# Graph attention in four layers: attention logits from 8-column products ahead of the value projection

## The chip, the cores and the metric

The kernel runs on one core of a Trainium2 chip. The metric is the device time of one execution in microseconds (us), taken as the median of several runs. A core has a matrix engine (TensorE, PE in the profile, with its weight loads shown apart as PEld), a vector engine (VectorE, DVE), a scalar engine for functions of one argument (ScalarE, ACT), a general engine (GpSimd, POOL) and a queue that issues transfers (SyncE, SP). Each runs its own instructions in the order in which they were written and waits on semaphores for the others. Products land in PSUM[...]; everything else lies in SBUF.

## The reference

Sixteen graphs of 1024 nodes with 256 features, each with a 0/1 adjacency matrix, go through four layers of graph attention. Every layer first normalises the features and clips them at zero, and adds its result to its input:

```python
h = jnp.maximum(_layernorm(x, axis=-1), 0.0)
x = x + _L0_gnn_ref(h, adj, L0_gnn_W, L0_gnn_a)
```

Within a layer, with H heads (4, 4, 4, 1) of 256/H columns:

```python
h = (x @ W)                                   # the values
s1 = einsum('bhnd,hd->bhn', h, a1)            # one number s per node and head
s2 = einsum('bhmd,hd->bhm', h, a2)            # one number d per node and head
e = leaky_relu(s1[:, :, :, None] + s2[:, :, None, :], slope)
e = where(adj == 0, -inf, e)
out = einsum('bhnm,bhmd->bhnd', softmax(e), h)
```

Layer 2 adds a bias, a clip, the values and a second normalisation over each head. Layer 3 has one head of 256 columns. All in float32.

## The kernel before, in words

*Numbers of a node.* The weights `wa[layer]` hold, per head, the columns of W and two more: W times a1 and W times a2 (line 579; folded in `weights`, lines 685 to 689). One product of the normalised features with `wa` so gives values and the logits' s and d together: 4 x 66 = 264 columns for four heads, 258 for one. Since a leaky ReLU of a sum is a maximum of two sums, the exponential of a logit can be written as a factor of the column node times (a row value relative to a threshold, clipped at zero, plus a constant). The factors `fac` (per column node) and the `rows` (per row node, spread over all partitions) come from s and d, less their maxima over all nodes.

*Units and tiles.* A unit is one layer of one graph. The 48 units of layers 0 to 2 stand in an order `main`, two graphs interleaved; each has 32 tiles (4 heads x 8 blocks of 128 column nodes). A tile goes through three engines: ACT makes `r` of 128 x 1024 in PSUM (`weigh`, line 991; two buffers), DVE adds, multiplies by the mask and writes `p` to SBUF (`cover`, line 1009; 13 buffers), PE multiplies `p` with the values `v` into `po` (`gather`, line 1075). `evacuate` and `finish` divide by the sums and update `x_cur`, the latter on POOL. The 16 units of layer 3 (`last_layer`, line 1178; `last_sums`, line 1193) run beside the tiles of other units.

*Preparing a unit* (`prepare`, line 801) starts at the earliest AHEAD = 60 tiles before its first tile and after the graph's former layer is finished. DVE takes the statistics (`st`), POOL turns them into offset and scale (`rs`), and then for four pairs of blocks (`normal`, line 750): POOL writes `hn`, PE transposes it, ACT clips it into `hT` (three buffers), and two `project` jobs (line 777) multiply `hT` with `wa` into a PSUM bank and copy the result to `v`. When the last of eight blocks is copied (`not u.left`, line 853), DVE reduces s and d over the node blocks (tile `wide`), PE transposes that, DVE reduces to the maximum over all nodes (`top`), PE spreads it with a product with `ones`, and DVE computes the exponents (`c`, `arg`) from s and d. ACT takes exponentials into `wide` (row side) and `fac`. The row side is transposed and goes through DRAM (`line`) to be read back over all partitions as `rows`; the very first unit and the last unit of layer 3 make it with PE instead (`direct`, line 917). In layers 0 and 1, POOL multiplies the values by a factor (`flatten`, line 959); otherwise it sets the column of ones in `v`.

*Order.* The file holds a planner (class `Plan`, line 417; main loop, line 1343): at build time it runs through all jobs with assumed durations (`cost`, line 437), picks for each engine among the jobs that can start first (within NEAR = 60 ns) the one with the smallest `until`, and emits instructions in that order. A preparation's `until` is the number of its unit's first tile; a gather's is the current tile plus SLACK = 36. Copies marked EITHER go to ACT as long as it isn't a nanosecond count of 10^9 behind DVE (DVE_MORE, line 389), which means always. PSUM has two banks `pp` for transposes, projections, the small products and the last layer's sums, two of twice the size for `r`, and two for `po`.

Of the kernel before, what the change touches and what calls it, by code (L numbers as in the profile page):

```python
# [20 lines left out]
P = 128  # L21
# [388 lines left out]
POOL_LATE = 100.0  # L410
LANES = 2


# [3 lines left out]
class Plan:  # L417
# [19 lines left out]
    def cost(self, engine: str, op: str, a: tuple, k: dict):  # L437
        size = lambda ap: math.prod(ap.shape[1:])
        aps = [v for v in (*a, *k.values()) if hasattr(v, "shape")]
        n = max(size(v) for v in aps)  # L440
        if engine == "PE":
            out, left = a[0], a[1]
            wide = size(left) > 64
            swap = 110.0 if self.mode not in (None, wide) else 0.0
            self.mode = wide
            if op == "transpose":
                return swap + (110.0 if left.dtype == F32 else 56.0), PE_LATE
            if left.dtype != F32:
                return swap + 57.0, PE_LATE
            return swap + max(59.0, size(out) * 0.833 + 3.0), PE_LATE  # L450
        if op == "dma_start":
            total = math.prod(a[0].shape) * mybir.dt.size(a[0].dtype)
            return (600.0 if engine == "POOL" else 400.0), 2200.0 + total / 180.0
        given = sum(size(v) == 1 for v in aps)
        if engine == "ACT":
            if n == 1024:
                return (1041.0 if "accum_out" in k else (903.0, 1050.0, 1143.0)[given]), ACT_LATE
            if n <= 64:
                return 100.0 + 0.7 * n, ACT_LATE
            return 50.0 + 0.833 * n + 114.0 * given + (40.0 if given == 2 else 0.0), ACT_LATE  # L460
# [48 lines left out]
def fast_path(  # L509
# [44 lines left out]
    WIDTH = [F // n + 2 for n in HEADS]  # L554
    VW = max(n * w for n, w in zip(HEADS, WIDTH))
    MAXN = max(HEADS)
# [193 lines left out]
    def normal(e, rs: bass.AP):  # L750
# [20 lines left out]
        else:  # L771
            dve.tensor_scalar(e.hT, ph.rearrange("p k i n -> p k (i n)"), 0.0, None, ALU.max)
        left()
        for i in range(2):
            add(u.until, project(e, i), plan.now)

    def project(e, i: int):

        u = e.u
        width = u.n * (u.w + 2)  # L780
        yield "PE", lambda: u.layer in folded and free_for(u) and max(folded[u.layer], free_for(u))
        pv, left = bank_for(u)
        for k in range(KC):
            for c in range(0, P, P // 2):
                at = i * P + c
                pe.matmul(
                    pv[c : c + P // 2, :width],
                    e.hT[:, k, at : at + P // 2],
                    wa[u.layer][:, k, :, :].rearrange("p h e -> p (h e)"),
                    start=(k == 0),  # L790
                    stop=(k == KC - 1),
                )
        e.left -= 1
        e.read = plan.now
        yield EITHER, None
        either_copy(u.v[:, 2 * e.pair + i, :width], pv[:, :width])
        left()
        u.left -= 1
        u.there = plan.now

    def prepare(u: "Unit"):

        n, w, layer = u.n, u.w, u.layer
        slope = SLOPE[layer]
        width = n * (w + 2)
        yield "DVE", lambda: (
# [7 lines left out]
        else:  # L814
            u.v = units.tile([P, NB, width], F32, name="v_one", bufs=1)
        v = u.v[:, :, :width].rearrange("p b (h e) -> p b h e", h=n)
        plan.now = max(plan.now, u.g.here)
        xt = u.g.x
        st = small.tile([P, NB, 2, 3], F32, name="st", bufs=2)
        for i in range(NB):  # L820
# [4 lines left out]

        rs = small.tile([P, 6, NB], F32, name="rs", bufs=2)
        m0, m1, q0, q1 = st[:, :, 0, 1], st[:, :, 1, 1], st[:, :, 0, 2], st[:, :, 1, 2]
# [9 lines left out]
        for pair in range(NB // 2):  # L837
            yield "POOL", lambda: (
                (len(pairs) < TURNS or pairs[-TURNS].turned)
                and (len(pairs) < PAIRS or not pairs[-PAIRS].left)  # L840
                and max(
                    1.0,
                    pairs[-TURNS].turned if len(pairs) >= TURNS else 0.0,
                    pairs[-PAIRS].read if len(pairs) >= PAIRS else 0.0,
                )
            )
            e = Unit()
            e.u, e.pair, e.turned, e.left = u, pair, False, 2
            pairs.append(e)
            g = normal(e, rs)  # L850
            add(u.until, g, 0.0, next(g))

        yield "DVE", lambda: not u.left and u.there
        s, d = (v[:, :, :, w + c].rearrange("p b h -> p h b") for c in range(2))

# [4 lines left out]
        mx = mine[:, 1, : 2 * n].rearrange("p (c h) -> p c h", c=2)  # L860
        dve.tensor_reduce(mx, v[:, :, :, w : w + 2].rearrange("p b h c -> p c h b"), AX.X, ALU.max)
        yield "PE", free_bank
# [11 lines left out]
        yield "DVE", None  # L874
        c = small.tile([P, 7, MAXN], F32, name="c", bufs=2)
        S, D, t, c1, c2, b1, b3 = (c[:, i, :n] for i in range(7))
# [82 lines left out]
    def flatten(u: "Unit", v: bass.AP):  # L959

        flat = u.fac[:, 2].rearrange("p h b -> p b h")
        for b in range(0, NB, 2):
# [28 lines left out]
    def weigh(u: "Unit", h: int, j: int):  # L991

        r, k = wide_bank()
        base = -1.0 if u.shared else u.fac[:, 3, h, j : j + 1]
        act.activation(r, u.row[h][0], AF.Relu, bias=base, scale=u.fac[:, 1, h, j : j + 1])
        weighed.append((u, None, h, j, r, k, plan.now))

    def weigh_some(u: "Unit", i: int, j: int):
# [5 lines left out]
        for k in range(MANY):  # L1004
            scale = u.fac[:, 1, 0, j + k : j + k + 1]
            act.activation(r[:, k], of, AF.Relu, bias=u.fac[:, 3, 0, j + k : j + k + 1], scale=scale)
        weighed.append((u, i, 0, j, r, at, plan.now))

    def cover():
# [3 lines left out]
        if i is None:  # L1013
            base = 1.0 if u.shared else u.fac[:, 2, h, j : j + 1]
            dve.scalar_tensor_tensor(by_blocks(p), by_blocks(r), base, mask(u.g, j), ALU.add, ALU.mult)
            covered.extend((u, c, h, j, p[:, c * half_n : (c + 1) * half_n], k, plan.now) for c in range(2))
        else:
            p_holds[k] = MANY
            p = p.rearrange("p (k n) -> p k n", k=MANY)
            for c in range(MANY):  # L1020
                m = mask(u.g, j + c)[:, i]
                dve.scalar_tensor_tensor(p[:, c], r[:, c], u.fac[:, 2, h, j + c : j + c + 1], m, ALU.add, ALU.mult)
                u.ps.append((p[:, c], k, plan.now))
# [4 lines left out]
    def make_whole(u: "Unit", h: int, j: int):  # L1028

        p, k = numerators()  # L1030
        whole[0] += 1
        base = -1.0 if u.shared else u.fac[:, 3, h, j : j + 1]
        act.activation(p, u.row[h][0], AF.Relu, bias=base, scale=u.fac[:, 1, h, j : j + 1])
        yield "POOL", None
        pool.tensor_scalar(p, p, 1.0 if u.shared else u.fac[:, 2, h, j : j + 1], 1.0, ALU.add, ALU.mult)
        yield "POOL", None
# [38 lines left out]
    def gather():  # L1075
# [7 lines left out]
        po = g[0]  # L1083
        at = h * (w + 2)
        for q in range(QUAD):
# [42 lines left out]
    def finish(u: "Unit", h: int, att, total):  # L1128

        n, w = u.n, u.w  # L1130
        at = h * (w + 2)
        wide = lambda ap: ap.unsqueeze(2).to_broadcast([P, NB, w])
# [134 lines left out]
    for b in range(G):  # L1267
# [4 lines left out]
        for layer in range(LAYERS):  # L1272
            u = Unit()
            u.g, u.layer, u.n, u.w = g, layer, HEADS[layer], F // HEADS[layer]
            u.finished, u.row, u.weighed, u.spent, u.left = {}, [], 0, False, NB
            u.ps = []
# [207 lines left out]
```

## Time and profile before

| | us |
|---|---|
| median of 3 runs (lowest, highest) | 3018.09 (3017.86, 3025.92) |
| the profiled execution's own time | 3014.36 |
| its span, from first to last instruction | 3012.4 |
| PE busy | 2694.6 |
| DVE busy | 2650.3 |
| ACT busy | 2414.9 |
| POOL busy | 1571.0 |
| value projection on PE (matmuls on `wa` and `hT`) | 518.3 |

All times in the profile are us, unless ns stands there. A group line names line, engine, operation, what is written and read, the shape, the count, then the busy time and the mean of one in ns, then the engine's idle time just before those instructions and who ended it. Nearly all instructions carry line 487, the helper that the planner calls them through, so groups are told apart by tile names. A line of waits has the waiting engine and tile, the releaser, total us, count and longest. A line of the timeline has the start, the time from the first start to the last end, engine, operation and count. A float32 product of 64 output rows shows as two matmuls and two weight loads.

### The profile page before, as it was taken

The page shows a single profiled execution, that of the slowest core. Times are in us where ns is not written, and L with a number is a line of the kernel's source. Part 1 is how long each engine was busy: PE and PEld are TensorE (multiplying, and loading weights), DVE is VectorE, ACT ScalarE, POOL GpSimd, SP SyncE. Part 2 cuts the span into 40 slices and gives each one's busy share as a digit, 9 for nine tenths or more (in the row PEclk, how much of TensorE's full clock was granted, in tenths as well). Part 3 has the DMA queues.
Part 4 walks back from the last instruction along what each step waited for, and adds up shares of the span by engine and source line. Part 5 has one row for each costly group of instructions (what it writes and reads, how often), then busy time and mean ns, then how long its engine had stood idle before and what let it go on. Part 6 is the DMA issues. An engine that isn't in the chain of part 4 may idle for free.

```text
span 3012.4 us, 130240 instructions
## 1 busy us (share of the span) xinstructions
PE 2694.6 (89%) x58915; PEld 2262.8 (75%) x58915; DVE 2650.3 (88%) x4065; ACT 2414.9 (80%) x3201; POOL 1571.0 (52%) x2263
## 2 busy tenths in 40 slices
PE   5888889999998989999898998989989899999867
PEld 4777777787776778778787786878778778887745
DVE  5889899899978989898998989989898998999963
ACT  5898888888878788888879788897888879878641
POOL 3445682754736447375463745637375464463630
PEclk8999999999999999999999999999999999999978
DMA  7323211323122131413113141321413213111100
GB/s 139 73 59 73 64 36 55 70 65 83 52 52 74 64 68 55 90 44 82 52 63 76 38 96 38 78 59 61 83 42 80 57 62 73 49 48 49 39 12 28
DMA packets 144292, 186.91 MB, mean 62 GB/s; under 512 B 80760, under 2 KB 116336, under 8 KB 142704
## 3 DMA queue, kind: packets, MB, share of 16 engines
q1 hardware_dynamic: 141680, 161.71, 18.5%
q0 software_dynamic: 2048, 16.78, 5.7%
q8 instruction: 464, 7.60, 1.0%
q14 instruction: 100, 0.82, 0.1%
HBM read 194.38 MB, written 34.40 MB: 76 GB/s over the span
## 4 chain that ended last, share of the span: by engine, by line
PE 35%; DVE 29%; ACT 21%; POOL 7%; issue 5%; DMA 1%; SPq 0%; ACTq 0%; POOLq 0%; DVEq 0%
DVE p L487 19%; PE pp L487 19%; PE po L487 16%; ACT r L487 15%; DVE st L487 3%; POOL att L487 2%; ACT seen L487 2%; DVE att L487 2%; ACT att L487 1%; DVE s L487 1%; DVE c L487 1%; POOL rs L487 1%; POOL hn L487 1%; ACT v L487 1%; ACT hT L487 1%
## 5 line engine op out<-in xcount | busy, mean ns | idle before, releaser
L487 ACT ACTIVATE r<-rows,fac 128x1024 f32<-128x1024 f32 (+1 forms) x1552 | 1766.0, 1148 | 363.3 <-DVE p L487 339.3
L487 PEld LDWEIGHTS po<-v,p 128*64 128x64 f32 x49216 | 1598.1, 140 | 332.4 <-DVE p L487 150.6
L487 PE MATMUL po<-v,p 128*64 128x65 f32 x49216 | 1665.0, 225 | 202.0 <-DVE p L487 128.7
L487 DVE SCALAR_TENSOR_TENSOR p<-r,mask 128x1024 f32<-128x1024 f32 x1024 | 1220.5, 1217 | 112.2 <-ACT r L487 86.8
L487 DVE SCALAR_TENSOR_TENSOR p<-r,fac,mask 128x1024 f32<-128x1024 f32 (+1 forms) x768 | 817.9, 1098 | 88.3 <-ACT r L487 71.0
L487 PE MATMUL pp<-wa,hT 128*64 128x264 f32 (+1 forms) x4056 | 518.3, 391 | 13.6 <-ACT hT L487 10.2
L487 POOL TENSOR_TENSOR att<-att,inv 128x512 f32<-128x512 f32 x128 | 133.9, 1046 | 744.6 <-DVE inv L487 628.3
L487 PE MATMUL pp<-v_one,p 128*64 128x257 f32 x3584 | 430.7, 383 | 2.7 <-DVE p L487 1.8
L487 PEld LDWEIGHTS pp<-wa,hT 128*64 128x64 f32 x4056 | 269.3, 138 | 138.9 <-ACT hT L487 16.5
L487 PEld LDWEIGHTS pp<-v_one,p 128*64 128x64 f32 x3584 | 267.2, 138 | 95.2 <-DVE p L487 9.0
L487 POOL TENSOR_SCALAR hn<-x_cur,rs 128x256 f32<-128x256 f32 x512 | 281.6, 562 | 36.4 <-PE pp L487 22.3
L487 PE MATMUL pp<-ident,hn 128*128 128x128 f32 x1020 | 178.8, 295 | 63.5 <-POOL hn L487 51.8
L487 POOL TENSOR_TENSOR x_cur<-att,x_cur 128x512 f32<-128x512 f32 x190 | 226.3, 1191 | 14.9
L487 ACT ACTIVATE r<-rows_one,fac 128x512 f32<-128x512 f32 x240 | 183.4, 778 | 19.3 <-DVE p L487 9.9
L487 PEld LDWEIGHTS pp<-ident,hn 128*128 128x128 f32 x1020 | 108.4, 143 | 120.3 <-POOL hn L487 91.9
L487 DVE BATCH_NORM_STATS2 st<-x_cur 128x6 f32<-128x256 f32 x512 | 180.8, 410 | 11.9 <-DMA x_cur<-in_x_dram 10.2
L487 ACT ACTIVATE hT<-pp 128x512 f32<-128x512 f32 x255 | 147.7, 594 | 39.3 <-PE pp L487 37.9
L487 ACT COPY v<-pp 128x264 f32<-128x264 f32 (+1 forms) x395 | 146.3, 383 | 21.1 <-PE pp L487 18.9
L487 POOL TENSOR_TENSOR v<-v,fac 128x512 f32<-128x512 f32 x128 | 136.1, 1088 | 47.3 <-ACT fac L487 47.3
L487 POOL TENSOR_TENSOR att<-att,s 128x512 f32<-128x512 f32 x124 | 133.1, 1074 | 10.0
L487 ACT ACTIVATE seen<-mask 128x1024 bf16<-128x1024 fp8e4 x128 | 134.6, 1052 | 0.4
L487 POOL TENSOR_TENSOR rs<-st 128x8 f32<-128x8 f32 x192 | 37.9, 211 | 153.9 <-DVE st L487 138.8
(91 smaller groups left out, 1616.3 us busy)
## 6 DMA issues: line engine op xcount, KB each, us to landing
rows<-line SPq DMA_DIRECT2D x191, 512.0 KB
x_cur<-in_x_dram SPq DMA_DIRECT2D x32, 512.0 KB
near<-in_adj_dram POOLq DMA_DIRECT2D x64, 256.0 KB, 8.1
out_dram<-y SPq DMA_DIRECT2D x128, 128.0 KB
rows_one<-line SPq DMA_DIRECT2D x15, 512.0 KB
mask<-near SPq DMA_TRANSPOSE x64
wa<-in_L_gnn_W_dram SPq DMA_DIRECT2D x6, 128.0 KB
line<-row SPq DMA_DIRECT2D x48, 16.0 KB
```

The source lines that it names most:

```text
L487: r = call(*a, **k)
```

## The change

The value projection no longer carries s and d. A new job `logits` runs once per pair, right after `hT`: eight products of `hT` with the two extra columns of every head (8 columns in layers 0 to 2, 2 in layer 3), all into one bank, one copy to a new small tile `sd`. The two `project` jobs of the pair multiply with the value columns alone (256), copy to `v`, and get an `until` that lies BEHIND = 16 tiles later. The maximum and the exponents read `sd` and wait for the four logits jobs (`u.begun == NB`) in place of the values. What needs the values on POOL (`flatten`, or the column of ones) waits for them there; `u.ready`, which lets ACT begin the unit's tiles, is set before that. `v` has one column per head less, `fac` one plane less (its unused first), `st`, `rs` and `c` have a third buffer. The planner's assumed cost of a product of at most 16 columns goes from 59 to 30 ns.

```diff
+BEHIND = 16
...
-            return swap + max(59.0, size(out) * 0.833 + 3.0), PE_LATE
+            return swap + (30.0 if size(out) <= 16 else max(59.0, size(out) * 0.833 + 3.0)), PE_LATE
...
-    VW = max(n * w for n, w in zip(HEADS, WIDTH))
+    VW = max(n * (w - 1) for n, w in zip(HEADS, WIDTH))
...
+        add(u.until, logits(e), plan.now)
         for i in range(2):
-            add(u.until, project(e, i), plan.now)
+            add(u.until + BEHIND, project(e, i), plan.now)
+
+    def logits(e):
+
+        u = e.u
+        yield "PE", lambda: u.layer in folded and free_for(u) and max(folded[u.layer], free_for(u))
+        pd, left = bank_for(u)
+        pd = pd[:, : 2 * 2 * u.n].rearrange("p (i h c) -> p i h c", i=2, c=2)
+        for i in range(2):
+            for k in range(KC):
+                for c in range(0, P, P // 2):
+                    at = i * P + c
+                    pe.matmul(
+                        pd[c : c + P // 2, i],
+                        e.hT[:, k, at : at + P // 2],
+                        wa[u.layer][:, k, :, u.w :],
+                        start=(k == 0 and i == 0),
+                        stop=(k == KC - 1),
+                        skip_group_check=True,
+                    )
+        e.left -= 1
+        e.read = plan.now
+        yield EITHER, None
+        either_copy(u.sd[:, 2 * e.pair : 2 * e.pair + 2], pd)
+        left()
+        u.begun += 2
+        u.known = plan.now
 
     def project(e, i: int):
...
+        pv = pv[:, :F].rearrange("p (h e) -> p h e", h=u.n)
...
-                    pv[c : c + P // 2, :width],
+                    pv[c : c + P // 2, :],
                     e.hT[:, k, at : at + P // 2],
-                    wa[u.layer][:, k, :, :].rearrange("p h e -> p (h e)"),
+                    wa[u.layer][:, k, :, : u.w],
...
-        either_copy(u.v[:, 2 * e.pair + i, :width], pv[:, :width])
+        either_copy(u.v[:, 2 * e.pair + i, : u.n * (u.w + 1)].rearrange("p (h e) -> p h e", h=u.n)[:, :, : u.w], pv)
...
+        u.sd = small.tile([P, NB, n, 2], F32, name=f"sd{n}", bufs=3)
...
-        st = small.tile([P, NB, 2, 3], F32, name="st", bufs=2)
+        st = small.tile([P, NB, 2, 3], F32, name="st", bufs=3)
...
-            e.u, e.pair, e.turned, e.left = u, pair, False, 2
+            e.u, e.pair, e.turned, e.left = u, pair, False, 3
...
-        yield "DVE", lambda: not u.left and u.there
-        s, d = (v[:, :, :, w + c].rearrange("p b h -> p h b") for c in range(2))
+        yield "DVE", lambda: u.begun == NB and u.known
+        s, d = (u.sd[:, :, :, c].rearrange("p b h -> p h b") for c in range(2))
...
-        dve.tensor_reduce(mx, v[:, :, :, w : w + 2].rearrange("p b h c -> p c h b"), AX.X, ALU.max)
+        dve.tensor_reduce(mx, u.sd.rearrange("p b h c -> p c h b"), AX.X, ALU.max)
...
-        u.fac = small.tile([P, 4, n, NB], F32, name=f"fac{n}", bufs=3)
+        u.fac = small.tile([P, 3, n, NB], F32, name=f"fac{n}", bufs=3)
...
-            act.activation(u.fac[:, 1:3], arg[:, 1:3], AF.Exp)
-            yield "POOL", None
+            act.activation(u.fac[:, 0:2], arg[:, 1:3], AF.Exp)
+            if not u.shared:
+                yield "POOL", None
+                pool.tensor_scalar(u.fac[:, 2], u.fac[:, 1], -1.0, 0.0, ALU.mult, ALU.add)
+            u.ready = plan.now
+            yield "POOL", lambda: not u.left and u.there
             if u.shared:
                 add(u.until, flatten(u, v), plan.now)
             else:
                 pool.memset(v[:, :, :, w], 1.0)
-                pool.tensor_scalar(u.fac[:, 3], u.fac[:, 2], -1.0, 0.0, ALU.mult, ALU.add)
                 u.flat = plan.now
-            u.ready = plan.now
```

The remaining edits follow the new numbering of `fac` and the narrower `v`.

More of the change, by code (lines that the diff above doesn't have):

```diff
@@ L773, in normal @@
         left()
+        add(u.until, logits(e), plan.now)
         for i in range(2):
-            add(u.until, project(e, i), plan.now)
+            add(u.until + BEHIND, project(e, i), plan.now)
[23 more added lines that the diff above has]
+        u.known = plan.now
     def project(e, i: int):
         u = e.u
-        width = u.n * (u.w + 2)
         yield "PE", lambda: u.layer in folded and free_for(u) and max(folded[u.layer], free_for(u))
         pv, left = bank_for(u)
+        pv = pv[:, :F].rearrange("p (h e) -> p h e", h=u.n)
         for k in range(KC):
@@ L804, in prepare @@
         slope = SLOPE[layer]
-        width = n * (w + 2)
+        width = n * (w + 1)
         yield "DVE", lambda: (
@@ L824, in prepare @@
         yield "POOL", None
-        rs = small.tile([P, 6, NB], F32, name="rs", bufs=2)
+        rs = small.tile([P, 6, NB], F32, name="rs", bufs=3)
         m0, m1, q0, q1 = st[:, :, 0, 1], st[:, :, 1, 1], st[:, :, 0, 2], st[:, :, 1, 2]
@@ L874, in prepare @@
         yield "DVE", None
-        c = small.tile([P, 7, MAXN], F32, name="c", bufs=2)
+        c = small.tile([P, 7, MAXN], F32, name="c", bufs=3)
         S, D, t, c1, c2, b1, b3 = (c[:, i, :n] for i in range(7))
@@ L959, in flatten @@
     def flatten(u: "Unit", v: bass.AP):
-        flat = u.fac[:, 2].rearrange("p h b -> p b h")
+        flat = u.fac[:, 1].rearrange("p h b -> p b h")
         for b in range(0, NB, 2):
@@ L993, in weigh @@
         r, k = wide_bank()
-        base = -1.0 if u.shared else u.fac[:, 3, h, j : j + 1]
-        act.activation(r, u.row[h][0], AF.Relu, bias=base, scale=u.fac[:, 1, h, j : j + 1])
+        base = -1.0 if u.shared else u.fac[:, 2, h, j : j + 1]
+        act.activation(r, u.row[h][0], AF.Relu, bias=base, scale=u.fac[:, 0, h, j : j + 1])
         weighed.append((u, None, h, j, r, k, plan.now))
@@ L1004, in weigh_some @@
         for k in range(MANY):
-            scale = u.fac[:, 1, 0, j + k : j + k + 1]
-            act.activation(r[:, k], of, AF.Relu, bias=u.fac[:, 3, 0, j + k : j + k + 1], scale=scale)
+            scale = u.fac[:, 0, 0, j + k : j + k + 1]
+            act.activation(r[:, k], of, AF.Relu, bias=u.fac[:, 2, 0, j + k : j + k + 1], scale=scale)
         weighed.append((u, i, 0, j, r, at, plan.now))
@@ L1013, in cover @@
         if i is None:
-            base = 1.0 if u.shared else u.fac[:, 2, h, j : j + 1]
+            base = 1.0 if u.shared else u.fac[:, 1, h, j : j + 1]
             dve.scalar_tensor_tensor(by_blocks(p), by_blocks(r), base, mask(u.g, j), ALU.add, ALU.mult)
@@ L1021, in cover @@
                 m = mask(u.g, j + c)[:, i]
-                dve.scalar_tensor_tensor(p[:, c], r[:, c], u.fac[:, 2, h, j + c : j + c + 1], m, ALU.add, ALU.mult)
+                dve.scalar_tensor_tensor(p[:, c], r[:, c], u.fac[:, 1, h, j + c : j + c + 1], m, ALU.add, ALU.mult)
                 u.ps.append((p[:, c], k, plan.now))
@@ L1031, in make_whole @@
         whole[0] += 1
-        base = -1.0 if u.shared else u.fac[:, 3, h, j : j + 1]
-        act.activation(p, u.row[h][0], AF.Relu, bias=base, scale=u.fac[:, 1, h, j : j + 1])
+        base = -1.0 if u.shared else u.fac[:, 2, h, j : j + 1]
+        act.activation(p, u.row[h][0], AF.Relu, bias=base, scale=u.fac[:, 0, h, j : j + 1])
         yield "POOL", None
-        pool.tensor_scalar(p, p, 1.0 if u.shared else u.fac[:, 2, h, j : j + 1], 1.0, ALU.add, ALU.mult)
+        pool.tensor_scalar(p, p, 1.0 if u.shared else u.fac[:, 1, h, j : j + 1], 1.0, ALU.add, ALU.mult)
         yield "POOL", None
@@ L1083, in gather @@
         po = g[0]
-        at = h * (w + 2)
+        at = h * (w + 1)
         for q in range(QUAD):
@@ L1130, in finish @@
         n, w = u.n, u.w
-        at = h * (w + 2)
+        at = h * (w + 1)
         wide = lambda ap: ap.unsqueeze(2).to_broadcast([P, NB, w])
@@ L1274, in fast_path @@
             u.g, u.layer, u.n, u.w = g, layer, HEADS[layer], F // HEADS[layer]
-            u.finished, u.row, u.weighed, u.spent, u.left = {}, [], 0, False, NB
+            u.finished, u.row, u.weighed, u.spent, u.left, u.begun = {}, [], 0, False, NB, 0
             u.ps = []
```

## The prediction

> **What bounds the kernel now.** I read the page first: shares, chain, groups.
>
> ```profile
> span 3012.4 us, 130240 instructions
> PE 2694.6 (89%) x58915; PEld 2262.8 (75%) x58915; DVE 2650.3 (88%) x4065; ACT 2414.9 (80%) x3201; POOL 1571.0 (52%) x2263
> PE 35%; DVE 29%; ACT 21%; POOL 7%; issue 5%; DMA 1%; SPq 0%; ACTq 0%; POOLq 0%; DVEq 0%
> L487 PE MATMUL pp<-wa,hT 128*64 128x264 f32 (+1 forms) x4056 | 518.3, 391 | 13.6 <-ACT hT L487 10.2
> ```
>
> No engine bounds it alone: three stand at 80 to 89%, and the chain that ended last changes between them. The fourth line is the value projection that the change splits. So I cut one period of the steady part (181 us, from 2187.9 to 2369.2: three units of heads and one last layer) into stretches of 7.5 us; five of them:
>
> ```profile
> core 0: us, PE busy (x) PEld busy (x) DVE busy (x) ACT busy (x) POOL busy (x), PEclk, DMA share, GB/s
> 2202.90:2210.40 7.50, 7.50 (x129) 5.55 (x127) 7.47 (x9) 7.22 (x11) 4.28 (x9) 1.00 0.01 2
> 2307.90:2315.40 7.50, 7.50 (x109) 5.22 (x103) 6.26 (x6) 6.96 (x12) 7.07 (x17) 1.00 0.60 105
> 2315.40:2322.90 7.50, 7.50 (x126) 5.85 (x126) 6.48 (x14) 7.50 (x12) 2.18 (x4) 1.00 0.77 81
> 2345.40:2352.90 7.50, 6.90 (x175) 5.89 (x171) 4.86 (x8) 7.36 (x14) 2.23 (x2) 1.00 0.21 77
> 2352.90:2360.40 7.50, 4.02 (x54) 2.43 (x54) 6.23 (x9) 7.47 (x11) 0.00 (x0) 0.89 0.00 0
> ```
>
> The first three hold preparations of a next unit (transposes, hT, values): PE is full and ACT nearly. The last two hold none: PE has room, ACT has not.
>
> Then the waits: is a unit's preparation ever late?
>
> ```profile
> ACT r L487 <- DVE c L487: 7.9, 4, 5.3
> ACT r L487 <- DMA rows<-line: 4.8, 1, 4.8
> DVE wide L487 <- ACT v L487: 36.9, 10, 17.0
> ```
>
> ACT waits 12.7 us in all for a unit's row or factors. The third line, the wait that the change shortens (the maximum over the logits waits for the last value), has two long members, seen in order of time at both ends:
>
> ```profile
> 28.27 0.27 DVE L487 TENSOR_REDUCE wide<-v 128x8 f32<-128x64 f32 x1 [17.05 <-ACT v L487]
> 35.96 2.15 ACT L487 ACTIVATE r<-rows,fac 128x1024 f32<-128x1024 f32 x2 [4.59 <-DVE rows L487]
> 2935.82 0.18 DVE L487 TENSOR_REDUCE wide<-v 128x2 f32<-128x16 f32 x1 [16.75 <-ACT v L487]
> ```
>
> Those two are 33.8 of the 36.9 us: in the steady part the wait is worth 3 us.
>
> **What the Trainium skill says.** "TensorE: Matmul & The Clock Gate", "Wait — 56ns, not 53.3ns?": start to start never drops below about 25 ns, however few columns. The trace agrees: the four 8-column products that exist already start their weight loads at 2396.34, and the next group starts at 2396.46, so 30 ns each, as long as a 65-column one (10.48 us for 350: 29.4 ns):
>
> ```profile
> 2396.34 0.25 PEld L487 LDWEIGHTS pp<-wide,ones 128*64 128x64 f32 x4
> 2339.40 10.48 PE L487 MATMUL po<-v,p 128*64 128x65 f32 x350
> 2967.09 31.38 PE L487 MATMUL pp<-v,p 128*64 128x257 f32 x288
> ```
>
> "Perfetto Trace Analysis", "Identifying the Most-Contended Engine": [...]weight-load busy is the better measure; here 75% against 89%. My own count lies between: a period holds 3072 instructions of 65 columns at 29.4 ns, 256 of 257 columns at 108 ns (31.38 us for 288), 256 of values at about the same 108 (16 in 2.00 us), and 64 transposes at 117 (8 in 1.09 us): 90 + 28 + 28 + 7 = 153 us of 181, 85%. The same page, "Optimization Strategy": where regimes have different contended engines, interleaving them can help. That is what speaks for the change.
>
> **The change, part by part.** Per unit (there are 64):
>
> *Added on PE*: four pairs x 8 products. A product of this type shows as two instructions (2048 value products show as 4056 + 40), so 64 per unit, 4096 in all. At 30 ns, 122.9 us. The planner's new price of 30 ns per product is half of that. Below 25 ns each (the page's floor) it can't go: 102 us; alone on a waiting PE, as at 29.82 (four in 0.29 us, one of 0.19), they take 33 ns: 135 us.
>
> *Removed on PE*: values lose 8 columns in layers 0 to 2 (3072 instructions) and 2 in the last (1024). From the two rows above, (108 - 29.4)/192 = 0.41 ns per column: 10.1 + 0.8 = 10.9 us. Net +112 us, 1.75 us per unit.
>
> *Added on ACT*: 256 copies of 16 (or 4) columns; copies always go to ACT, since DVE_MORE is 1e9. Nearest rows: small ACTIVATEs of 32 and 8 columns at 229 and 209 ns; take 210: +54 us. "ScalarE: Activation LUTs", "What ACT_TABLE_LOAD costs", gives 186 + 0.833 per column and 93 ns overlap back to back, an estimate of 106 ns: +27 us is the low end. Narrower value copies save nothing visible (383 ns for 264, 382 for 258).
>
> *DVE and POOL*: the same operations read sd in place of v; 0. A smaller stride could help the reads a little or not at all; I take 0, between -6 and +6 us (40 ns either way on some 150 reads of median 210 ns). u.ready no longer waits for POOL, so ACT may start a unit sooner; nothing waited for it. The memset and flatten move behind the values, on POOL, which idles 48%; behind them in its queue stand hn and att work. If values come within 5 us of the unit's first gather, the flatten (4 x 1.06 us) would delay PE; that cover is now about 15 us or more (fac at 2402.4, its unit from about 2425).
>
> *Banks*: four more holders of a pp bank per unit, some 1.2 us each, 307 us on two banks. PE now waits 14.5 + 5.5 us for banks or hT; below 10 us more.
>
> *No DMA is added*; row and rows follow their logits sooner, still limited by three row buffers. The third st, rs and c buffers remove no wait that the trace shows; 0.
>
> *What reaches the end.* PE carries 35% of the chain, ACT 21%: 112 x 0.35 + 54 x 0.21 = 39 + 11 = 50 us. Off it: both ends. At the start the last hT is ready at 24.8 and the maximum starts at 28.27; without values in between the transposes also come sooner: I take 4 us. At the end the fourth pair still waits for the first pair's values (three hT buffers): its logits would be there at about 2931.8 in place of 2935.8: 4 us. BEHIND lets gathers go before values until 20 tiles ahead of the unit in place of 36, and so takes value work (64 instructions x 108 ns = 6.9 us per unit) out of the full stretches where a later one has room. Of four preparations in a period, only the last stretch above offers 3.5 us of room: half of that, 1 us a period net of its disorder, 15 periods: -5 to -15, I take 5. Sum: 3014.4 + 50 - 8 - 5 = 3051 for the profiled execution (its own time, 2 us above its span). The median of the runs is 3.7 us above it: 3055.
>
> **The rivals.** *A, likeliest, 0.57*: as summed; 3030 to 3085.
>
> *B, PE becomes the bound, 0.15*: the PE work lands in full where PE is full, and three of four preparations fall there: 3018 + 0.75 x 112 - 8 = 3094; with all of it, 3122. For it: the full stretches above. Against it: up to 13 tiles of numerators lie between DVE and PE, and PE is at 85% by my count.
>
> *C, faster, 0.18*: the deferral empties the full stretches. Per period the logits cost 4 x 1.75 = 7 us of PE, of which three preparations, 5.3 us, lie in full stretches. If more than one unit's values in four (6.9 us) move to where PE has room, it wins; with 8 to 9 us moved, 3 us less a period in part, about -15 us, and -8 at the ends: 2995. For it: PE at 4.0 of 7.5 us at 2353. Against it: ACT is full just there, and value copies are ACT's work.
>
> *D, hidden, 0.10*: PE's idle 318 us take all, the ends pay for ACT: 3018. "It doesn't do what it says" is in D too: logits earlier, but rows held by their three buffers, as the 12.7 us of waits suggest.
>
> **How the numbers follow.** The forecast is A, 3055. The range, 2990 to 3097, takes in C's centre, D and B's near half; outside lie B's rest (0.08) and C's (0.09). Measurement tells 0.3%, 9 us. A and B are slower but for 0.02 of A: slower 0.70. C gives faster 0.17 (0.01 of it same). D 0.10 + 0.02 + 0.01: same 0.13.
>
> **What would show it.** A group of 8-column matmuls on wa and hT, about 3072 instructions, 30 ns apart; PE busy near 2805 and ACT near 2465; a copy to sd of about 210 ns, 256 times; the first numerators' ACTIVATE at about 32 in place of 35.96; periods of about 184 in place of 181 us. Wrong: if 8-column products run two abreast below 20 ns, or if the PE-full stretches get shorter than before, C holds; if DVE waits for PE (13.2 us now) several times longer, B.

## The result and the profile after

The changed kernel takes 3033.83 us (median of 5 runs, 3030.89 to 3035.45) against 3018.09 us beside it: a ratio of 1.0053, 95% interval 1.0039 to 1.0067. It is slower by 16 us, and not by the 37 that the prediction gave.

The page after, shares of the engines and the chain that ended last:

```profile
span 3032.6 us, 138694 instructions
PE 2780.8 (92%) x63011; PEld 2388.5 (79%) x63011; DVE 2641.9 (87%) x4065; ACT 2441.1 (80%) x3457; POOL 1571.8 (52%) x2263
PE 56%; DVE 18%; ACT 17%; issue 5%; POOL 3%; DMA 1%; SPq 0%; ACTq 0%; DVEq 0%; POOLq 0%
```

The chain has moved to PE: 56% in place of 35%. The most useful reading is a subtraction. PE is busy 86.2 us longer than before (2780.8 - 2694.6), but its idle time fell from 317.8 us (3012.4 - 2694.6) to 251.8 (3032.6 - 2780.8), so by 66.0. The span is the sum of both: +20.2 us. The added work is there; something gave most of it back.

The groups that the change made, kinds of shape kept apart:

```profile
L488 PE MATMUL pp<-wa,hT 128*64 128x256 f32 x4064 | 520.4, 383 | 5.3 <-ACT v L488 2.2 <-DVE y L488 0.8 <-issue 0.7
L488 PE MATMUL pp<-wa,hT 128*64 128x8 f32 x3024 | 113.8, 202 | 7.3 <-ACT hT L488 6.4 <-ACT sd L488 0.6
L488 PE MATMUL pp<-wa,hT 128*64 128x2 f32 x1024 | 39.0, 200 | 1.2 <-ACT hT L488 1.2
L488 ACT COPY sd<-pp 128x16 f32<-128x16 f32 x189 | 31.9, 176 | 25.4 <-PE pp L488 24.9
L488 ACT COPY sd<-pp 128x4 f32<-128x4 f32 x64 | 10.8, 168 | 9.9 <-PE pp L488 9.6
```

The 8-column instructions are as many as counted (3024 here, 48 more in the `r` banks). A copy to `sd` takes 176 ns.

PE's waits in the kernel before; the columns are total us, how often, and the longest:

```profile
PE po L487 <- DVE p L487: 128.7, 96, 12.0
PE pp L487 <- POOL hn L487: 51.8, 32, 15.3
PE po L487 <- issue: 20.5, 24, 3.5
PE pp L487 <- ACT hT L487: 14.5, 18, 2.2
```

The same view of the changed kernel:

```profile
PE po L488 <- DVE p L488: 79.9, 81, 14.7
PE po L488 <- issue: 35.7, 30, 3.3
PE pp L488 <- POOL hn L488: 34.8, 19, 15.1
PE pp L488 <- ACT hT L488: 12.0, 25, 2.5
```

Here is where the 66 us of idle time went: 48.8 us less waiting for numerators `p` and 17.0 less for `hn`. (Waits for the next instruction to be issued rose by 15.2; smaller waits fell by about as much.)

Where the time was lost is told by when units end. Each of the 48 units of four heads ends its tests with one reduction on DVE; these are the tenth and the forty-seventh in the timeline of before:

```profile
628.53 0.27 DVE L487 TENSOR_REDUCE greatest<-inv 128x1 f32<-128x32 f32 x2
2846.62 0.27 DVE L487 TENSOR_REDUCE greatest<-inv 128x1 f32<-128x32 f32 x2
```

and in that of the changed kernel:

```profile
646.02 0.26 DVE L488 TENSOR_REDUCE greatest<-inv 128x1 f32<-128x32 f32 x2
2864.10 0.27 DVE L488 TENSOR_REDUCE greatest<-inv 128x1 f32<-128x32 f32 x2
```

Between these the two kernels take 2218.09 and 2218.08 us: the steady part comes out even. 17.5 us are lost in the first ten units, 2.7 in the tail. (With the same two orders and other masks, further down, these are 2218.02 and 2218.54 us, and 14.3 us for the first ten units.)

The same cuts in windows show why. After the length stand the busy times of PE, PEld, DVE, ACT and POOL, then the granted clock, the DMA share and GB/s. Before:

```profile
0.00:628.53 628.53, 531.11 (x12145) 449.37 (x12147) 540.00 (x817) 514.40 (x694) 337.57 (x493) 0.98 0.31 72
628.53:2846.62 2218.09, 2043.88 (x45243) 1726.66 (x45237) 2017.59 (x3057) 1843.10 (x2428) 1194.08 (x1709) 0.99 0.25 62
```

and in the changed kernel:

```profile
0.00:646.02 646.02, 555.03 (x13081) 483.36 (x13082) 543.76 (x820) 522.96 (x752) 336.52 (x493) 0.98 0.31 70
646.02:2864.10 2218.08, 2100.55 (x48340) 1816.15 (x48338) 2006.66 (x3057) 1859.68 (x2620) 1196.48 (x1710) 1.00 0.25 63
```

In the first ten units PE is busy 23.9 us longer, and its idle time falls only from 97.4 to 91.0 us. In the steady part it is busy 56.7 us longer, and its idle time falls by just as much, from 174.2 to 117.5.

Last, the two ends, where the forecast saw 8 us to gain. From the timeline after:

```profile
27.61 0.27 DVE L488 TENSOR_REDUCE wide<-sd 128x8 f32<-128x64 f32 x1 [16.08 <-ACT sd L488]
35.52 2.15 ACT L488 ACTIVATE r<-rows,fac 128x1024 f32<-128x1024 f32 x2 [3.11 <-DVE rows L488]
54.12 2.78 DVE L488 BATCH_NORM_STATS2 st<-x_cur 128x6 f32<-128x256 f32 x8 [8.45 <-DMA x_cur<-in_x_dram]
2963.65 1.60 ACT L488 ACTIVATE r<-rows,fac 128x512 f32<-128x512 f32 x2 [4.31 <-DVE inv L488]
```

At the start the maximum comes 0.66 us sooner, the first `r` 0.44 us, and then DVE, in order, waits for the second graph's `x_cur`, which lands when it lands (54.12; before 53.27). At the end the last unit's `r` comes 20.7 us later than before, while the last unit of four heads ends 17.0 later: nothing gained there either.

### The profile page after: what moved, and what is told of

Its sections match the earlier page's. It is cut to its first block, busy times and chain, and to the rows that moved or that the text cites. A ratio compares the mean times of both kernels' runs of the same rounds, so it can differ in the third digit from the quotient of the medians.

```text
span 3032.6 us, 138694 instructions
## 1 busy us (share of the span) xinstructions
PE 2780.8 (92%) x63011; PEld 2388.5 (79%) x63011; DVE 2641.9 (87%) x4065; ACT 2441.1 (80%) x3457; POOL 1571.8 (52%) x2263
## 4 chain that ended last, share of the span: by engine, by line
PE 56%; DVE 18%; ACT 17%; issue 5%; POOL 3%; DMA 1%; SPq 0%; ACTq 0%; DVEq 0%; POOLq 0%
PE po L488 29%; PE pp L488 27%; ACT r L488 12%; DVE p L488 11%; ACT seen L488 2%; DVE st L488 2%; DVE att L488 2%; ACT hT L488 1%; ACT att L488 1%; DVE c L488 1%; POOL att L488 1%; DMA x_cur<-in_x_dram 1%; DVE s L488 1%; ACT v L488 1%; DVE y L488 1%
## 5 line engine op out<-in xcount | busy, mean ns | idle before, releaser
L488 PE MATMUL po<-v,p 128*64 128x65 f32 x49216 | 1668.4, 224 | 158.0 <-DVE p L488 79.9
L488 PE MATMUL pp<-wa,hT 128*64 128x256 f32 (+2 forms) x8112 | 662.3, 292 | 13.8 <-ACT hT L488 7.6
L488 PEld LDWEIGHTS pp<-wa,hT 128*64 128x64 f32 x8112 | 427.2, 138 | 120.3 <-ACT hT L488 15.9
L488 PE MATMUL pp<-ident,hn 128*128 128x128 f32 x1020 | 176.0, 292 | 45.8 <-POOL hn L488 34.8
L488 ACT COPY v<-pp 128x256 f32<-128x256 f32 x396 | 146.2, 374 | 81.4 <-PE pp L488 80.4
L488 ACT COPY att<-po 128x260 f32<-128x260 f32 x256 | 93.2, 375 | 47.2 <-PE po L488 43.0
```

The costliest lines, as they stand in the source:

```text
L488: r = call(*a, **k)
```

## The experiments

Three theories stood at the outset. *Share*: the added work costs about its engine's share of the chain (the forecast). *Cancel*: the added work costs nearly in full, and the later values give most of it back. *Room and order*: what is seen is mostly a different plan, and added work fits into idle time. A word on names: "the load" is eight 8-column products per pair of blocks, as the change adds them.

**The load alone, in the order of before.** The products go to columns of the values' bank that nobody reads, and are issued past the planner, so no other instruction moves:

```diff
+        for k in range(KC):
+            for c in range(0, P, P // 2):
+                at = i * P + c
+                nc.tensor.matmul(pv[c : c + P // 2, 496 : 496 + 2 * u.n],
+                    e.hT[:, k, at : at + P // 2], wa[u.layer][:, k, :, u.w :], ...)
```

> The kernel before with 8 unused products of 8 (or 2) columns per pair put in front of the value products into spare columns of their bank, past the planner, so that every engine's order stays that of before; values keep their 264 columns. It adds 4096 matmul instructions on PE and nothing else. Theory 'share' (the forecast's: added PE work costs by PE's share of the chain, whatever the order): 123 x 0.35 = 43 us longer, about 3061. Theory 'cancel' (added work does cost, the deferral of the values gives it back): also longer, by 25 to 50 us, a three-unit period of 183 us or more in place of 181. Theory 'room and order' (PE has room in the steady part; what was lost comes from another order of the work in the first 650 us and at the end): under 12 us longer, period 181 to 182.

Measured: 3118.14 us (3116.28 to 3124.34), 1.0339 of before (1.0325 to 1.0353), so +101 us on 3016.72. That is 82% of the 123 us of instructions. The page:

```profile
span 3117.8 us, 138430 instructions
PE 2820.4 (90%) x63011; PEld 2395.8 (77%) x63011; DVE 2647.4 (85%) x4065; ACT 2427.8 (78%) x3201; POOL 1573.5 (50%) x2263
PE 52%; DVE 21%; ACT 15%; POOL 7%; issue 4%; DMA 1%; SPq 0%; ACTq 0%; POOLq 0%; DVEq 0%
```

PE is busy 125.8 us longer and idle 297.4: only 20 us of the load went into idle time. *Share* (43 us) and *room* (less than 12) fall.

**The copies on top.** The same, with one ScalarE copy of 16 (or 4) columns per pair:

```diff
+        if i:
+            extra = small.tile([P, 4 * MAXN], F32, name="extra", bufs=3)
+            nc.scalar.copy(extra[:, : 4 * u.n], pv[:, : 4 * u.n])
```

> As x1_load, and one copy of 16 (or 4) columns per pair on ACT, to a small unused tile, behind the second value copy of the pair: all the added work of the change on PE and ACT, at the order of before. 'Share': 43 + 256 x 0.176 x 0.21 = 52 us longer. 'Cancel': longer than x1_load by 5 to 15 us. 'Room and order': within 6 us of x1_load.

Measured: 3120.05 us, 1.034 (1.0326 to 1.0355). The copies cost 2 us, which is no difference that these runs can tell from nothing.

**The change without its deferral.**

```diff
-BEHIND = 16
+BEHIND = 0
```

> The changed kernel with BEHIND = 0: values no longer deferred, logits still ahead. 'Share' with a small gain from deferral: 5 us longer than the changed kernel, 3039. 'Cancel': the steady period rises from 181 to 183 us or more, 3060. 'Room and order': period stays at 181 to 182; the total moves by up to 15 us to either side of 3034, by where the first 650 us and the end fall.

Measured: 3093.53 us (3089.35 to 3104.43), 1.0269 (1.0248 to 1.029). So +77 on the kernel before, and 60 us above the change. *Cancel* was the nearest theory, and it had 3060. The waits of PE say what is different from the change:

```profile
PE po L488 <- DVE p L488: 91.0, 91, 15.3
PE pp L488 <- ACT hT L488: 47.6, 35, 2.8
PE pp L488 <- POOL hn L488: 33.2, 7, 15.6
PE pp L488 <- ACT v_one L488: 24.8, 9, 3.3
```

The waits for `p` are already shorter than before (128.7), but new ones stand in their place: 47.6 us for `hT` (12.0 in the change) and 24.8 for a bank. By the timeline (further down), with values and logits equally urgent a preparation runs as a tight chain of transposes, `hT` and products, with nothing between.

**Plans alone.** The kernel before with the price of 30 ns and the third `st`, `rs` and `c` buffers, no work added:

```diff
-            return swap + max(59.0, size(out) * 0.833 + 3.0), PE_LATE
+            return swap + (30.0 if size(out) <= 16 else max(59.0, size(out) * 0.833 + 3.0)), PE_LATE
...
-        st = small.tile([P, NB, 2, 3], F32, name="st", bufs=2)
+        st = small.tile([P, NB, 2, 3], F32, name="st", bufs=3)
...
```

> The kernel before with only those parts of the change that add no work: the planner's price of 30 ns for products of at most 16 columns, and third buffers of st, rs and c. The instructions are the same, their order is planned anew. 'Share' and 'cancel': within 4 us of before, since no work is added. 'Room and order': it may move by 5 to 15 us to either side although nothing is added, most of it before 650 us.

Measured: 3011.72 us, 0.9978 (0.9967 to 0.999): a new plan by itself moves 5 us.

Next, what the changed order is bound by, and whether deferral needs the early logits.

**The products doubled**, in the changed kernel's order, the second set into spare columns of the bank:

```diff
+        for i in range(2):
+            for k in range(KC):
+                for c in range(0, P, P // 2):
+                    at = i * P + c
+                    nc.tensor.matmul(spare[c : c + P // 2, i], e.hT[:, k, at : at + P // 2], wa[u.layer][:, k, :, u.w :], ...)
```

> The changed kernel with the eight products of every logits job issued twice, the second time into columns of the same bank that nobody reads; the order of all the rest is the changed kernel's, so TensorE gets 4096 more 8-column instructions, about 123 us. 'Cancel' (added work costs nearly in full, the deferred values gave it back; TensorE is the bound of the steady part either way): +80 to +123 us over the changed kernel, about 3125, some 2 us per unit from the ninth on. If instead the deferral has made room on TensorE (the changed kernel's steady part is bound by DVE or ACT), the first 40 us or so are free: below 3085.

Measured: 3164.08 us, 1.0475 (1.046 to 1.049) of its own before. That is 130 us above the change for 4096 instructions, 31.8 ns each: the full price, with no idle time taken at all (253.6 us are left: span 3168.8 less 2915.2). In the changed order PE's added work lands in full.

**Deferral without early logits.** The kernel before, its projections due 16 tiles later:

```diff
-            add(u.until, project(e, i), plan.now)
+            add(u.until + 16, project(e, i), plan.now)
```

> The kernel before with one edit: the projection jobs, which still carry s and d, get an until that lies 16 tiles later, so the logits wait with them. 'Cancel', strong form: putting value work later is worth its 60 us by itself wherever the logits come from: 2950 to 2975. Weak form: the deferral only pays because the logits no longer wait for it; here the rows and factors come up to 16 tiles later and ACT waits for them: 3000 to 3040, with waits of ACT's r for rows or factors above the 13 us of before. 'Room and order' has no view but that any new order is within 12 us of 3017.

Measured: 3011.44 us, 0.9972 (0.9959 to 0.9984): 8 us faster than before, little more than the 5 us of the new plan above. The strong form falls. The weak form has the time right but not its reason: ACT's waits for rows are 13.8 us, not longer than before.

**The planner's price.** The change with 59 in place of 30 ns for small products:

```diff
-            return swap + (30.0 if size(out) <= 16 else max(59.0, size(out) * 0.833 + 3.0)), PE_LATE
+            return swap + max(59.0, size(out) * 0.833 + 3.0), PE_LATE
```

> The changed kernel with the planner's price of a small product back at 59 ns, which is what a product (two instructions of 30 ns) takes. If the remaining 16 us come from a plan that thinks TensorE 61 us freer than it is: faster than the changed kernel, 3000 to 3025. If the price does not matter, within 10 us of 3034. The planner spreads work differently, so part of any difference up to 12 us may be order alone (the run with the price and the buffers alone moved 5).

Measured: 3044.65 us, 1.0084 (1.007 to 1.0098), some 11 us slower than the change, at the edge of the second expectation. The halved price was not what cost time.

**More deferral.**

```diff
-BEHIND = 16
+BEHIND = 24
```

> The changed kernel with BEHIND at 24 in place of 16. With 0 it took 3094, with 16 3034: 60 us for 16 tiles. 'Cancel' with more to give: 3005 to 3030. If the gain is used up at 16 (gathers can go before values only until SLACK, 36, less BEHIND tiles ahead; with 24 the values come within 12 tiles of their unit): 3030 to 3045. If values come late for their gathers: above 3050, with TensorE waiting for ACT's v or ACT's r for po.

Measured: 3059.7 us, 1.0138 (1.0122 to 1.0153): 26 us slower than with 16, as the third expectation had it, but not by the waits that it named: PE waits 47.1 us for `hn` (34.8 with 16) and 87.3 for `p` in place of 79.9. More deferral is not better.

**Six runs with plain mask transfers.** The remaining runs load the masks untransposed, by transfers of the same size:

```diff
-sp.dma_start(g.edges[:, q, :], near[:, q * P : (q + 1) * P], transpose=True)
+sp.dma_start(g.edges[:, q, :], near.rearrange("(q p r) c -> q p (r c)", p=P, r=2)[q])
```

Each tile then gets other 0/1 values, so the output is not the reference's, and four of these runs are measured against two footings of the same kind.

> A footing for the three runs beside it: the kernel before with the masks loaded by plain transfers of the same size instead of transposing ones, so every tile gets other 0/1 values and the output is not the reference's; all engines' instructions and their order are those of before. Masks are fetched far ahead and DMA carries 1% of the chain: within 6 us of before, 3012 to 3024, by every theory.

> The second footing: the changed kernel with the masks loaded by plain transfers, with the same effect on the output. The difference to the kernel before with plain transfers should be that of the result, 10 to 22 us; the time 3026 to 3040.

Measured: 3019.62 (1.0001 of before, 0.9993 to 1.0009) and 3035.88 (1.0058, 1.0039 to 1.0078). Both stand where they stood with transposed masks.

**Half of the logits products**, the second 128 features left out, the order kept:

```diff
+                    if k:
+                        plan.spend("PE", 30.0, PE_LATE)
+                        continue
```

> The changed kernel with plain mask transfers, in its own order, and half of the logits products left out: only the first 128 of the 256 features enter s and d, so logits are partial sums. TensorE loses 2048 8-column instructions, about 61 us. If the changed order is bound by TensorE (doubling the products cost 130 us for 123), the loss returns in full: 58 to 65 us below the changed kernel with plain transfers, about 2973. If TensorE is only just the bound, DVE or ACT takes over after the first 20 us or so: 3010 to 3020.

Measured: 2993.76 us, 0.9913 (0.9898 to 0.9927): 42 us below its footing for 61 us of instructions. It lies between the two expectations. Added work costs 106% of its instructions' time in this order, taken-away work returns 69%. The page's busy times and its chain:

```profile
PE 2731.1 (91%) x60963; PEld 2326.3 (78%) x60963; DVE 2636.4 (88%) x4065; ACT 2435.7 (81%) x3457; POOL 1575.9 (53%) x2263
PE 46%; DVE 22%; ACT 19%; POOL 6%; issue 5%; DMA 1%; SPq 0%; ACTq 0%; DVEq 0%; POOLq 0%
```

As PE gets freer, DVE and ACT return to the chain.

**Packing.** A narrow instruction costs about 30 ns at 8 columns and 29.4 at 65. So the logits job can take 64 value columns with it, nearly free, and the value jobs become 192 wide (`wa` is laid out with the logits columns first):

```diff
-                        wa[u.layer][:, k, :, u.w :],
+                        wa[u.layer][:, k, : own + FIRST],
...
+        either_copy(u.v[:, 2 * e.pair : 2 * e.pair + 2, :FIRST], pd[:, :, own:])
...
-                    wa[u.layer][:, k, :, : u.w],
+                    wa[u.layer][:, k, 2 * u.n + FIRST :],
```

> The changed kernel with plain mask transfers, the logits job made 64 value columns wider (72 columns, or 66 in the last layer), the value jobs 64 columns narrower (192), and one more copy of 2 x 64 columns per pair on ScalarE. By 30 ns at 8 columns, 29.4 at 65 and 108 at 257, an instruction of 72 columns takes about 32 ns and one of 192 about 82: TensorE loses 4096 x (108 - 82 - 2) = 98 us against the changed kernel. If TensorE is the bound of this order: 2935 to 2965. If ACT takes over (256 more copies of about 230 ns less 512 x 50 ns: +33 us): 2965 to 3010. If narrow products aren't what costs: above 3020.

Measured: 3020.63 us, 1.0002 (0.9992 to 1.0012). Only 15 us below its footing; but the planner had prices of its own for the new shapes and chose another order. So the same packing once more in exactly the changed kernel's order, the extra copy issued past the planner:

```diff
+            m = {72: 8, 66: 2, 192: 256}.get(size(out), size(out))
+            return swap + (30.0 if m <= 16 else max(59.0, m * 0.833 + 3.0)), PE_LATE
```

> The run before it with 72-column logits jobs and 192-column value jobs, but now in the changed kernel's own order: the planner is told the old prices, and the extra copy is issued past it. Masks by plain transfers, as in the footing of the changed kernel (3036). If the packing gave only 15 us because the planner chose another order: 2965 to 2995, as the 61 us of products left out gave 42. If the narrower instructions or the extra copies are themselves not worth it: 3010 to 3036 again.

Measured: 3000.88 us, 0.9942 (0.9926 to 0.9958). The same instructions gain 20 us more in the better order: 35 us below the footing of the change, 19 below that of before. That still misses the expectation (2965 to 2995): of the 98 us worked out, about a third returns. Its page:

```profile
span 2997.9 us, 139208 instructions
PE 2708.1 (90%) x63011; PEld 2375.0 (79%) x63011; DVE 2633.9 (88%) x4065; ACT 2451.8 (82%) x3713; POOL 1572.4 (52%) x2263
PE 39%; DVE 28%; ACT 24%; issue 5%; POOL 3%; DMA 1%; SPq 0%; ACTq 0%; DVEq 0%; POOLq 0%
```

PE lost 74 us of busy time against its footing (2782.5), and idle time rose by 38: DVE and ACT (with 256 copies more) take over. This is the fastest form seen that leaves no work out; it was not run with transposed masks.

**Deferral under the load, logits late.** The two edits shown above, projections due 16 tiles later and the unused products, made together on the kernel before, with plain masks:

> The kernel before with masks by plain transfers, its projection jobs (s and d still in them) 16 tiles later, and the eight unused 8-column products of the load experiment issued at each pair's values. Without the load this order takes 3011. If the deferral itself makes room for work on TensorE, the 123 us cost little: 3020 to 3060. If the room comes only with logits that do not wait for the values, the load costs what it cost in the order of before: 3011 + 100, 3105 to 3135.

Measured: 3100.6 us, 1.0273 (1.0256 to 1.029). The load costs 89 us here (3011.44 without it), just short of the second theory and far from the first. PE's waits:

```profile
PE po L487 <- DVE p L487: 125.7, 106, 12.5
```

PE waits for `p` as long as in the kernel before.

Four of the runs now make a table. All four carry the load; what differs is mainly the order (plain masks move a time by 2 us at most, so the plain run may stand in it):

| us | values not deferred | values deferred by 16 tiles |
|---|---|---|
| logits with or after the values | 3118.1 | 3100.6 |
| logits first | 3093.5 | 3033.8 |

Deferral alone gives 18 us, early logits alone 25, both together 84. The lower row also has the narrower values (11 us by the prediction's estimate), the planner's price and the third buffers (5 us on the kernel before), and the copies to `sd` (2 us), so less than 25 may belong to early logits. Neither edit has much worth by itself: with early logits the deferral gives 60 us, without them 18.

**What the pair does.** The traces show it in PE's idle stretches of 2 us or more between 650 and 2600 us: 13 before (41 us in all), 10 with the load in the old order (34 us), 26 with `BEHIND` at 0 (70 us), 9 with late logits deferred (35 us), 3 in the change (7 us; 8 and 18 us in its footing with plain masks). And such a stretch costs more than itself. From the run with `BEHIND` at 0, PE's timeline:

```profile
1131.21 0.69 PE L488 MATMUL po<-v,p 128*64 128x65 f32 x16
1134.05 0.63 PE L488 MATMUL pp<-ident,hn 128*128 128x128 f32 x4 [2.15 <-ACT hT L488]
1137.47 5.00 PE L488 MATMUL pp<-wa,hT 128*64 128x8 f32 x48 [2.80 <-ACT hT L488]
```

and most of it in windows of 3.41 us (columns as in the windows of the result):

```profile
1131.72:1135.13 3.41, 0.81 (x11) 0.46 (x6) 3.38 (x7) 3.34 (x7) 2.87 (x5) 1.00 0.29 51
1135.13:1138.55 3.42, 1.08 (x18) 1.08 (x20) 3.42 (x7) 3.39 (x6) 0.95 (x2) 0.50 0.00 0
1138.55:1141.96 3.41, 3.41 (x20) 1.89 (x20) 2.20 (x5) 2.04 (x4) 3.18 (x4) 0.50 0.02 5
```

PE is busy 0.81 us in the first window, and the granted clock is at half in the next; there PE is busy 1.08 us, and half the clock follows again. The 48 instructions of 8 columns take 5.00 us there. The kernel before has it too, after a wait for `p`:

```profile
994.37 3.65 PE L487 MATMUL pp<-v_one,p 128*64 128x257 f32 x32
1003.07 2.45 PE L487 MATMUL po<-v,p 128*64 128x65 f32 x48 [2.72 <-DVE p L487]
1005.30 4.49 PE L487 MATMUL pp<-v_one,p 128*64 128x257 f32 x32
```

and in windows:

```profile
1000.18:1003.59 3.41, 0.69 (x23) 0.56 (x21) 3.35 (x5) 2.78 (x3) 0.00 (x0) 1.00 0.11 35
1003.59:1007.00 3.41, 3.41 (x46) 2.69 (x44) 3.35 (x4) 3.08 (x4) 0.00 (x0) 0.50 0.14 52
1007.00:1010.41 3.41, 3.41 (x54) 2.50 (x52) 2.59 (x4) 3.09 (x3) 0.00 (x0) 1.00 0.27 102
```

The same 32 products take 3.65 us ahead of the idle stretch of 2.72 us and 4.49 after it.

These windows are the clock's own: in all sixteen traces its record has no value but full and half, and changes only on a grid of 3.41 us. What told half from full in these traces is how busy PE was in the window before, by the profile's busy times, and not the length of one stretch. Of the windows at full clock with PE busy for less than 40%, all 303 were followed by half; between 40% and 55% it was 78 of 254; above that, 17 of 12937. From half, the clock came back only after a window with PE busy for 76% or more (382 times). The Trainium skill, "TensorE: Matmul & The Clock Gate", "HAM oscillation — how this bites in real kernels", warns of idle gaps above about 3.4 us; here single stretches of 2.72 us, and of 2.15 us with the start of the next, were enough.

In the change the same phase looks like this on PE:

```profile
1131.33 0.63 PE L488 MATMUL pp<-ident,hn 128*128 128x128 f32 x4
1131.88 0.64 PE L488 MATMUL pp<-wa,hT 128*64 128x8 f32 x16
1132.37 1.13 PE L488 MATMUL po<-v,p 128*64 128x65 f32 x32
1133.33 0.59 PE L488 MATMUL pp<-wa,hT 128*64 128x8 f32 x16
1133.77 1.13 PE L488 MATMUL po<-v,p 128*64 128x65 f32 x32
1134.73 2.76 PE L488 MATMUL pp<-wa,hT 128*64 128x256 f32 x24
```

The logits products are short; gathers go between them, and the values, which nobody waits for yet, come after. Read with the table: deferred values serve as filler, but only once the logits no longer hang on them.

How much of the gain is clock can be estimated: the clock's shortfall times PE's busy time, summed over stretches of 5 us. It is 67 us with `BEHIND` at 0, 59 for the load in the old order, 54 for late logits deferred, 41 before (54 in its footing with plain masks, so it varies by 13), 29 in the change (32 in its footing, 48 with the products doubled). Of the 57 us of span between `BEHIND` at 0 and at 16, which run the same number of instructions, 33 are idle time (284.7 against 251.8) and 25 are a shorter busy time (2805.4 against 2780.8), which the clock's 38 us can account for. Of the 85 us of span between the load in the old order and the change, 46 are idle time (297.4 against 251.8) and 40 a shorter busy time (2820.4 against 2780.8), which the clock's 30 and the narrower values' 11 can account for. For the packed kernel in its own order the estimate is 54, in the changed kernel's order 32: about the 20 us between those two. This part was read from traces; no run held the clock fixed.

## Why the prediction was wrong

Its direction and range held, but by luck: its centre was only 21 us too high because two larger errors of opposite sign nearly cancel.

*The step that failed: "What reaches the end", 112 x 0.35 + 54 x 0.21 = 50.* The share of the chain was no price for work added on PE. In the order of before the load cost 101 us where that step gives 43 (123 x 0.35), and the copies 2 where it gives 11. PE's share rose from 35% to 52% as the load came: the chain moves to what is loaded. Rival B, that PE becomes the bound, was near the right price for this part (0.75 of the added time; 0.82 measured). What spoke against B was a count of 153 us in a period of 181, 85%; but PE is busy for 2043.88 of the 2218.09 us of the steady part, 92%.

*The step that failed beside it: the deferral, "I take 5".* With early logits it gave 60 us, and the whole order 84. The prediction looked for stretches with room (3.5 us in the last one, half of that taken) and found few. What it missed is that deferred values needn't find an empty stretch: they fill the gaps of 1 to 5 us where PE waits for `p` or `hn`, and, by the traces, they keep the clock up. It had the waits in hand: 128.7 and 51.8 us. Rival C came nearest to this mechanism, and put its break-even at 5.3 us a period. The order's 84 us over 15 periods are 5.6, and the steady part did come out even; but C asked for values moved to stretches with room, while what shrank was waits. The Trainium skill's "Perfetto Trace Analysis", "Optimization Strategy", on which C rested, advises interleaving where the contended engine changes. This case agrees as far as it goes: values spread among other work gave 60 us (`BEHIND` at 16 against 0), which the products took up again.

*The products' price* was near: 30 ns taken, 31.8 by doubling, in which the estimated shortfall of the clock rose from 29 to 48 us. *PE's busy time* was forecast near 2805 and came to 2780.8. By the estimates above, 12 of the missing 24 us are the better clock (29 against 41); the rest stays open. With `BEHIND` at 0 it is 2805.4, but with 26 us more of shortfall than before, so this is no proof that the sum of the work was right. The 10.9 us for narrower values are not visible in their group (518.3 before, 520.4 after).

*The copies* were put at 210 ns, 54 us in all, with an estimate of 27 as the low end. They take 176 and 168 ns, 43 us for the 253 on record, between the two. ACT's busy time rose by 26.2 us, but that can't decide it: in the load run without copies it also rose, by 12.9.

*ACT's waits* for a unit's row or factors were put at 12.7 us "in all". The same view of before also has `rows` from DVE (6.9 us) and `rows_one`, the last layer's row (5.3), so 24.9. They fell to 11.4, and nothing here shows that this moved the end.

*DVE, POOL, banks* at nothing or below 10 us: right. DVE's busy time fell by 8 us (forecast within 6), and PE's waits for banks or `hT` stayed where they were.

*The ends*, -8: not there. At the start the planner put the values of the first pairs between the transposes, and the first `r` gained 0.44 us in place of 4, which DVE's wait for `x_cur` then took away. At the end, values and a group of the last layer's sums stand ahead of the fourth pair's transposes.

*Periods* were to go from 181 to 184 us; they stayed at 181. Rival D's 3018 is nearest to the measured time, and idle time did take 66 of the 86 us, but D's reason falls: the idle time of the order before took 20 of 126 when it was offered the same load.

*What stays open* is why PE's idle time in the first ten units gave way by only 6.4 of 97.4 us. The products are what costs there: 896 of the 4096 instructions, 27 us at 30 ns; doubled, they cost 35.5 us more by the tenth unit, and halved, 15 less. The deferral doesn't help there: with `BEHIND` at 0 the tenth unit ends at 638.44, 7.6 us before that of the change.

## What to carry to other kernels

In this kernel, with three engines at 80 to 89%, work added on PE cost 82 to 106% of its own time, not its engine's share of the chain that ended last, while 256 short copies on ACT cost nothing that could be told. So don't take the share for a price; try the load alone, in the old order. A few dozen microseconds of waits on the same engine are what a new order can win, so cost the order separately. Work that nobody waits for soon was the best filler, so split what is urgent (a few columns) from what is not; but here an instruction of 8 columns cost as much as one of 65, so fill the narrow ones up. When a change moves the order, read the engine's idle time and the granted clock beside its busy time: the same instructions took 25 us less busy time in the better order.

## What was not expected of the hardware

An instruction of 8 columns costs 31.8 ns where PE is full, and one of 72 columns so little more that packing took PE's busy time down by 74 us. The granted clock answered to how busy PE was in windows of 3.41 us, so that idle stretches of 2 to 3 us could bring it to half. And PE's gathers waited 20.5 us (24 times) for issue before and 35.7 (30 times) in the change. The 4096 more instructions alone don't bring this about, since with `BEHIND` at 0 it is 17.5 us; what does was not tried.
